# Layer 0's experts in two runs of blocks that take turns, each with a weight buffer loaded where the expert changes

## The chip, the cores and the metric

The kernel runs on one core of a Trainium2 chip. The metric is the device time of one execution in microseconds, the median of a few runs; lower is better. The profile is one execution recorded by the hardware profiler.

## What is computed

The program is a decoder of four layers over 8 x 256 = 2048 tokens of width 256. Each layer has an attention, a cross-attention and a feed-forward part, each with a residual and a LayerNorm behind it. The change touches the feed-forward part of layer 0, a mixture of eight experts where each token goes to one expert:

```python
x_flat = x.reshape(-1, D)                        # 2048 x 256
router_logits = x_flat @ gate_w                  # 2048 x 8
router_probs = softmax(router_logits)
expert_idx = argmax(router_probs)
expert_w = router_probs[expert_idx]
for e in range(8):                               # w1[e]: 256 x 1024, w2[e]: 1024 x 256
    y = gelu(x_flat @ w1[e] + b1[e]) @ w2[e] + b2[e]
    out = out + where(expert_idx == e, expert_w, 0)[:, None] * y
...
x = layernorm(x + out)
```

## The kernel before

The tokens are kept as 16 tiles of 128 (`NT`), in `X` with tokens on the partitions and in `xT` with features there. `l0_ffn` works in three stages.

The router multiplies `xT` by the gate (`plog`), picks the best expert of each token, counts tokens per expert and gives each expert as many blocks of 128 slots as its tokens need. At most `NB` = 16 + 7 = 23 blocks can come up, and the loop always runs over 23. `end` holds the running sum of the blocks, `slot` says at which place each token stands, `take` (from `takers`) says which token stands at each place of each block. `owner` is the expert of each block times 128; blocks behind the last used one belong to expert 7. `wrow` adds the partition's number: it is, for each block, the list of 128 rows of the table `l0f_experts` that hold the weights of the expert. The tokens are also written to DRAM (`xd`).

The second stage is the loop over blocks. For block `n`, GpSimd issues an indirect DMA (`gather_rows`, line 893) that fetches 128 rows of 4360 numbers, the expert's `w1`, `w2`, `b1` and `b2`, into the tile `we`. The pool `f0e` has two buffers, so a load waits until the block before last has done its last read. A second indirect DMA (in `gathered_T`) fetches the 128 tokens of the block into `xe`; TensorE transposes them (`pt`, line 908), ScalarE copies the result to `xeT`. Then TensorE makes eight pieces of the hidden layer (`ph`), ScalarE applies Gelu with the bias `b1` (`hT`, line 999), TensorE multiplies by `w2` (`py`), VectorE adds `b2` (`y`, line 1005, the last read of `we`), and SP writes `y` to `yd` in DRAM. A matrix product in 32-bit floats shows as two matmuls in the trace, so a block has 32 rows of `ph` and 16 of `py`.

The third stage gathers from `yd` the row of each token (`yg`), scales it by the router's weight, adds the residual and normalises (`finish`).

The order of the instructions on each engine is chosen by a scheduler when the program is built; the source gives only the dependences. Each engine's queue runs in its order. On GpSimd's queue the built order is, once the loop has settled, one gather of `xe` and then one of `we`, and in the last seven turns `we` alone. `gather_rows` has an optional bound (`rows`): rows of the index at or above it are dropped and raise no error. Before the change only the lookup of layer 2's table (`rows` from `l2f_table`) passes one.

Of the kernel before, what the change touches and what calls it, by code (L numbers as in the profile page):

```python
# [11 lines left out]
F32 = mybir.dt.float32  # L12
# [4 lines left out]
ALU = mybir.AluOpType  # L17
# [3 lines left out]
P = 128  # L21
B, S, D = 8, 256, 256
# [20 lines left out]
class Net:  # L43
# [874 lines left out]
    def l0_ffn(self, w):  # L918
        nc, tc = self.nc, self.tc
        (gate,) = w  # L920
        E, FC = 8, 8
        NB = NT + E - 1
        with (
            tc.tile_pool(name="f0", bufs=1) as pool,
            tc.tile_pool(name="f0w", bufs=3) as work,
            tc.tile_pool(name="f0e", bufs=2) as ework,
            tc.tile_pool(name="f0d", bufs=1, space=bass.MemoryType.DRAM) as dram,
        ):
            with tc.tile_pool(name="f0r", bufs=1, space=PSUM) as ps:
                plog = ps.tile([P, NT, E], F32, name="plog")  # L930
                for i in range(NT):
                    self.mm(plog[:, i, :], [(self.xT4[:, c, i, :], gate[:, c, :]) for c in range(2)])
                m8, _, oh, pos, cnt = self.route(plog, E, 1, pool, ps)
                pe = pool.tile([P, NT, 8], F32, name="pe")
                nc.vector.tensor_tensor(pe, m8, m8[:, :, 0:1].to_broadcast([P, NT, 8]), ALU.subtract)
                nc.scalar.activation(pe, pe, AF.Exp)
                gw = pool.tile([P, NT], F32, name="gw")
                nc.vector.tensor_reduce(gw, pe, AX.X, ALU.add)
                nc.vector.reciprocal(gw, gw)
                nblk = pool.tile([P, E], I32, name="nblk")  # L940
                nc.vector.tensor_scalar(nblk, cnt, float(P - 1), None, ALU.add)
                nc.vector.tensor_single_scalar(nblk, nblk, 7, ALU.arith_shift_right)
                end = pool.tile([P, E + 1], F32, name="end")
                nc.vector.memset(end[:, 0:1], 0.0)
                for e in range(E):
                    nc.vector.tensor_tensor(end[:, e + 1 : e + 2], end[:, e : e + 1], nblk[:, e : e + 1], ALU.add)
                first = pool.tile([P, E], F32, name="first")
                nc.vector.tensor_scalar(first, end[:, :E], float(P), None, ALU.mult)
                slotf = pool.tile([P, NT, E], F32, name="slotf")
                nc.vector.tensor_tensor(slotf, pos, first.unsqueeze(1).to_broadcast([P, NT, E]), ALU.add)  # L950
            xd = self.in_dram(pool, dram)
            slot1 = self.pick(oh, slotf, 1, E, pool, "slot1")
            slot = pool.tile([P, NT, 1], U32, name="slot")
            nc.vector.tensor_copy(slot, slot1)
            parts = pool.tile([P, 2, NT, 1], I32, name="parts")
            nc.vector.tensor_single_scalar(parts[:, 0], slot.bitcast(I32), 7, ALU.arith_shift_right)
            nc.vector.tensor_single_scalar(parts[:, 1], slot.bitcast(I32), P - 1, ALU.bitwise_and)
            block = pool.tile([P, 2, NT, 1], F32, name="block")
            nc.vector.tensor_copy(block, parts)
            group = pool.tile([P, NT, 1, NB], F32, name="group")  # L960
            nc.vector.tensor_tensor(
                group[:, :, 0, :],
                self.cst("iota")[:, :NB].unsqueeze(1).to_broadcast([P, NT, NB]),
                block[:, 0].to_broadcast([P, NT, NB]),
                ALU.is_equal,
            )
            with tc.tile_pool(name="f0t", bufs=1, space=PSUM) as ps:
                take = self.takers(block[:, 1], group, 1, pool, work, ps, pool)
            past = pool.tile([P, NB, E], F32, name="past")
            nc.vector.tensor_tensor(  # L970
                past,
                self.cst("iota")[:, :NB].unsqueeze(2).to_broadcast([P, NB, E]),
                end[:, 1:].unsqueeze(1).to_broadcast([P, NB, E]),
                ALU.is_ge,
            )
            owner = pool.tile([P, NB], F32, name="owner")
            nc.vector.tensor_reduce(owner, past, AX.X, ALU.add)
            nc.vector.tensor_scalar(owner, owner, float(E - 1), float(P), ALU.min, ALU.mult)
            wrow = pool.tile([P, NB], U32, name="wrow")
            nc.vector.tensor_scalar(wrow, owner, self.cst("part"), None, ALU.add)  # L980
            yd = dram.tile([NB * P, D], F32, name="yd")
            with tc.tile_pool(name="f0p", bufs=2, space=PSUM) as ps:
                for n in range(NB):
                    we = ework.tile([P, 2 * FC * P + FC * D + FC + D], F32, name="we")
                    self.gather_rows(we, self.ins["l0f_experts"], wrow[:, n : n + 1])
                    o = 2 * FC * P
                    w1 = we[:, :o].rearrange("p (c f) -> p c f", c=2)
                    w2 = we[:, o : o + FC * D].rearrange("p (f d) -> p f d", d=D)
                    b1 = we[:, o + FC * D : o + FC * D + FC]
                    b2 = we[:, o + FC * D + FC :]  # L990
                    xeT = self.gathered_T(xd, take[:, n : n + 1], work)
                    hT = work.tile([P, FC, P], F32, name="hT")
                    for g in range(0, FC, 4):
                        ph = ps.tile([P, 4, P], F32, name="ph")
                        for f in range(4):
                            self.mm(
                                ph[:, f, :], [(w1[:, c, (g + f) * P : (g + f + 1) * P], xeT[:, c, :]) for c in range(2)]
                            )
                            nc.scalar.activation(  # L999
                                hT[:, g + f, :], ph[:, f, :], AF.Gelu, bias=b1[:, g + f : g + f + 1]  # L1000
                            )
                    py = ps.tile([P, D], F32, name="py")
                    self.mm(py, [(hT[:, f, :], w2[:, f, :]) for f in range(FC)])
                    y = work.tile([P, D], F32, name="y")
                    nc.vector.tensor_tensor(y, py, b2, ALU.add)  # L1005
                    nc.sync.dma_start(yd[n * P : (n + 1) * P, :], y)
                for i in range(0, NT, 2):
                    z = work.tile([P, 2, D], F32, name="z")
                    for j in range(2):
                        y = work.tile([P, D], F32, name="yg")  # L1010
                        self.gather_rows(y, yd, slot[:, i + j, :])
                        nc.vector.scalar_tensor_tensor(
                            z[:, j], y, gw[:, i + j : i + j + 1], self.X[:, i + j, :], ALU.mult, ALU.add
                        )
                    self.finish(i, 1, z)
# [1023 lines left out]
```

## Time and profile before

| | |
|---|---|
| three timed runs | 2792.59, 2801.1, 2802.07 us; median 2801.1 |
| the profiled execution | 2675.02 us, of which the span of the core is 2673.2 us |
| mean granted TensorE clock in it | 0.883 |
| the loop over blocks in it | first `ph` at 332.4 us, last `y` at 557.2 us |
| loads of `we` in it | 23, each 2.23 MB |
| one gather instruction of `we` on GpSimd | median 942 ns |
| one `y` on VectorE | 424 to 426 ns |

Durations in what follows come from this one execution. A row of the trace gives the start and the length, the engine, the line of the source, the operation and its tiles (output, arrow, inputs), and in brackets how long the engine stood idle before it and what ended that. PE is TensorE, PEld its weight loads, DVE VectorE, ACT ScalarE, POOL GpSimd, SP the engine that issues plain DMAs. A releaser named in brackets is inferred: of several things waited for, it is the one that came last by the profile. The table's lines of code are those of the kernel before.

### The profile page before, as it was taken

The page shows a single profiled execution, that of the slowest core. Times are in us where ns is not written, and L with a number is a line of the kernel's source. Part 1 is how long each engine was busy: PE and PEld are TensorE (multiplying, and loading weights), DVE is VectorE, ACT ScalarE, POOL GpSimd, SP SyncE. Part 2 cuts the span into 40 slices and gives each one's busy share as a digit, 9 for nine tenths or more (in the row PEclk, how much of TensorE's full clock was granted, in tenths as well). Part 3 has the DMA queues.
Part 4 walks back from the last instruction along what each step waited for, and adds up shares of the span by engine and source line. Part 5 has one row for each costly group of instructions (what it writes and reads, how often), then busy time and mean ns, then how long its engine had stood idle before and what let it go on. Part 6 is the DMA issues. An engine that isn't in the chain of part 4 may idle for free.

```text
span 2673.2 us, 40915 instructions
## 1 busy us (share of the span) xinstructions
PE 2156.6 (81%) x14331; PEld 1560.5 (58%) x14331; DVE 1678.8 (63%) x5710; ACT 957.6 (36%) x2197; POOL 890.1 (33%) x949
## 2 busy tenths in 40 slices
PE   8978688869999867854998667888898899878975
PEld 5555477745556546741555425666677677656754
DVE  4754400056666757536676788787797787664876
ACT  2321133323333344211344224345455445433431
POOL 1021121131111112446111003776767766670000
PEclk9998599989998877985999788898999998887987
DMA  2001276720001013743000001212111211220000
GB/s 84 2 1 36 88 255 242 268 76 1 1 1 68 13 43 99 229 147 87 1 1 25 36 0 60 54 52 53 51 48 46 59 46 50 54 75 0 1 20 12
DMA packets 84172, 166.28 MB, mean 62 GB/s; under 512 B 31653, under 2 KB 51253, under 8 KB 80256
## 3 DMA queue, kind: packets, MB, share of 16 engines
q0 software_dynamic: 52288, 110.51, 13.5%
q1 hardware_dynamic: 28924, 49.45, 5.5%
q10 hardware_dynamic: 2756, 3.72, 0.4%
q8 instruction: 114, 1.87, 0.3%
q14 instruction: 90, 0.74, 0.1%
HBM read 242.90 MB, written 17.70 MB: 97 GB/s over the span
## 4 chain that ended last, share of the span: by engine, by line
PE 20%; DVE 17%; DMA 6%; issue 5%; POOL 2%; ACT 2%; POOLq 0%; ACTq 0%; DVEq 0%
DMA rows<-in_l2f_table_dram,index 6%; PE s L132 3%; PE pp L132 3%; PE po L1392 3%; PE po L132 3%; DVE junk L1340 2%; DVE low L478 1%; POOL rows L893 1%; PE ph L132 1%; PE sc L132 1%; PE s L1538 1%; PE sc L445 1%; PE s L1516 1%; DVE X L187 1%; DVE top_i L1216 1%
## 5 line engine op out<-in xcount | busy, mean ns | idle before, releaser
L893 POOL DMA_INDIRECT rows<-in_l2f_table_dram,index x512 | 531.9, 1039 | 227.7 <-issue 68.9
L1340 DVE SCALAR_TENSOR_TENSOR junk<-rows,X 128x256 f32<-128x256 f32 x512 | 215.8, 421 | 145.7 <-DMA rows<-in_l2f_table_dram,index 134.6
L1392 PE MATMUL po<-rows,diag 128*128 128x256 f32 x768 | 218.5, 423 | 43.6 <-ACT diag L1391 41.6
L132 PE MATMUL ph<-xeT,we 128*128 128x128 f32 x1248 | 187.4, 294 | 35.2 <-DMA we<-in_l0f_experts_dram,wrow 31.0
L132 PEld LDWEIGHTS ph<-xeT,we 128*128 128x128 f32 x1248 | 172.8, 204 | 58.5 <-DMA we<-in_l0f_experts_dram,wrow 34.4
L1392 PEld LDWEIGHTS po<-rows,diag 128*128 128x128 f32 x768 | 149.0, 207 | 91.3 <-ACT diag L1391 65.0
L553 POOL TENSOR_TENSOR aT<-sides,inv 128x256 f32<-128x256 f32 x64 | 46.7, 730 | 448.4 <-DVE sides L551 255.8
L132 PE MATMUL pp<-xT,w 128*128 128x256 f32 (+1 forms) x672 | 183.4, 411 | 9.6 <-DVE hT L1028 3.3
L173 PE MATMUL pt<-ident,X 128*128 128x128 f32 x352 | 77.7, 335 | 119.7 <-DVE X L187 105.5
L1391 ACT ACTIVATE diag<-ident,dots 128x128 f32<-128x128 f32 x384 | 133.1, 394 | 103.0 <-DVE dots L1386 62.7
L893 POOL DMA_INDIRECT xe<-xd,take x87 | 85.0, 977 | 221.7 <-DVE y L1005 94.7
L132 PEld LDWEIGHTS pp<-xT,w 128*128 128x128 f32 x672 | 131.9, 203 | 40.2 <-issue 9.4
L174 ACT COPY xT<-pt 128x512 f32<-128x512 f32 x88 | 51.5, 586 | 277.0 <-PE pt L173 276.7
L1005 DVE TENSOR_TENSOR y<-py,we 128x256 f32<-128x256 f32 x23 | 9.8, 425 | 220.3 <-PE py L132 220.3
L141 POOL TENSOR_SCALAR rs_v<-ln_mv 128x2 f32<-128x2 f32 x48 | 12.4, 259 | 389.2 <-DVE ln_mv L164 358.5
L173 PEld LDWEIGHTS pt<-ident,X 128*128 128x128 f32 x352 | 50.2, 165 | 156.7 <-issue 73.3
L132 PE MATMUL py<-we,hT 128*128 128x256 f32 x496 | 132.2, 391 | 0.9 <-DVE hT L1028 0.9
L517 ACT ACTIVATE e<-sc 128x512 f32<-128x512 f32 (+1 forms) x155 | 82.0, 602 | 105.5 <-PE sc L445 92.2
L999 ACT ACTIVATE hT<-ph,we 128x128 f32<-128x128 f32 x184 | 66.0, 367 | 142.8 <-PE ph L132 136.0
L187 DVE TENSOR_SCALAR X<-z,ln_mv,rs_y 128x256 f32<-128x256 f32 x192 | 72.0, 418 | 52.2 <-POOL rs_y L143 52.1
L445 PE MATMUL sc<-kv,qv 32*128 32x128 f32 (+2 forms) x1448 | 101.5, 320 | 2.8 <-DVE sides L551 0.8
L445 PEld LDWEIGHTS sc<-kv,qv 32*128 32x128 f32 x1448 | 78.3, 190 | 37.4 <-issue 30.1
(489 smaller groups left out, 5223.5 us busy)
## 6 DMA issues: line engine op xcount, KB each, us to landing
we<-in_l1f_experts_dram SPq DMA_DIRECT2D x32, 384.0 KB, 4.2
yd<-y SPq DMA_DIRECT2D x32, 256.0 KB, 2.1
rows<-in_l2f_table_dram,index POOLq DMA_INDIRECT x512, 2.8
w<-in_l2x_w_dram SPq DMA_DIRECT2D x1, 4096.0 KB
yd<-y SPq DMA_DIRECT2D x23, 128.0 KB, 1.7
X<-in_x_dram SPq DMA_DIRECT2D x8, 256.0 KB, 7.7
xd<-X ACTq DMA_DIRECT2D x8, 256.0 KB, 2.2
xd<-X SPq DMA_DIRECT2D x8, 256.0 KB, 2.1
```

Of the source, the lines that this page charges most:

```text
L132: self.nc.tensor.matmul(out, lhsT=lhsT, rhs=rhs, start=n == 0, stop=n == last and bias is None)
L173: nc.tensor.transpose(pt[:, c, j, :], self.X[:, i0 + j * step, c * P : (c + 1) * P], self.ident)
L174: nc.scalar.copy(self.xT4[:, :, i0 : i0 + step + 1 : step, :], pt)
L187: nc.vector.tensor_scalar(self.X[:, i, :], z[:, j, :], mv[:, j, 0:1], r[:, j : j + 1], ALU.subtract, ALU.mult)
L445: nc.tensor.matmul(sc[: shape[0], part], lhsT=lhsT, rhs=rhs, start=mask is None, stop=True, skip_group_check=True)
L517: lambda r, sc: nc.scalar.activation(e0[m][:n0, r], sc, AF.Exp),
L553: nc.gpsimd.tensor_tensor(out, split(both), split(inv), ALU.mult)
L893: self.nc.gpsimd.indirect_dma_start(out=out, out_offset=None, in_=table, in_offset=bass.IndirectOffsetOnAxis(ap=index, axis=0), **({} if r ...
L999: nc.scalar.activation(hT[:, g + f, :], ph[:, f, :], AF.Gelu, bias=b1[:, g + f : g + f + 1])
L1340: nc.vector.scalar_tensor_tensor(junk, row, 1.0, self.X[:, i, :], ALU.mult, ALU.mult, accum_out=out)
L1391: nc.scalar.activation(diag, self.ident, AF.Copy, scale=dots[:, k : k + 1])
L1392: nc.tensor.matmul(po, lhsT=diag, rhs=rows[:, k, D:], start=False, stop=g + k == H * K - 2)
```

## The change

The blocks are cut into two runs, 0 to 11 and 12 to 22. The loop takes them in turns: 0, 12, 1, 13 and so on to 22, 11. Each run has a buffer of its own for weights, so the two tiles are allocated once by name instead of by a pool of two. A new vector `same` marks the blocks whose expert is that of the block before them, with the first block of each run unmarked; a million is added to the rows of the marked blocks in `wrow`. The gather is still issued at each turn, now with the bound of 1024 rows (`E * P`), so that the rows of a marked block are dropped and the buffer keeps the weights that it has.

```diff
-            tc.tile_pool(name="f0e", bufs=2) as ework,
...
             nc.vector.tensor_scalar(owner, owner, float(E - 1), float(P), ALU.min, ALU.mult)
+            first = (NB + 1) // 2
+            turns = [n // 2 + n % 2 * first for n in range(NB)]
+            same = pool.tile([P, NB], F32, name="same")
+            nc.vector.tensor_tensor(same[:, 1:], owner[:, 1:], owner[:, : NB - 1], ALU.is_equal)
+            for n in (0, first):
+                nc.vector.memset(same[:, n : n + 1], 0.0)
+            nc.vector.scalar_tensor_tensor(same, same, 1e6, owner, ALU.mult, ALU.add)
             wrow = pool.tile([P, NB], U32, name="wrow")
-            nc.vector.tensor_scalar(wrow, owner, self.cst("part"), None, ALU.add)
+            nc.vector.tensor_scalar(wrow, same, self.cst("part"), None, ALU.add)
+            weights = [pool.tile([P, 2 * FC * P + FC * D + FC + D], F32, name=f"we{n}") for n in range(2)]
...
-                for n in range(NB):
-                    we = ework.tile([P, 2 * FC * P + FC * D + FC + D], F32, name="we")
-                    self.gather_rows(we, self.ins["l0f_experts"], wrow[:, n : n + 1])
+                for turn, n in enumerate(turns):
+                    we = weights[turn % 2]
+                    self.gather_rows(we, self.ins["l0f_experts"], wrow[:, n : n + 1], E * P)
```

## The prediction

> **What bounds the kernel now.** I read the page's rows first, then who waits on the tile of weights, then TensorE and GpSimd in order of time within layer 0's experts, last the clock in short windows.
>
> The whole kernel leans on TensorE (first fence, the page's busy row and its queue row), but this change touches one stage of some 225 us, so the share of the span says nothing of it. The stage is closed off on both sides: the router must be done before the first gather, and the gathers of `yd` wait for every block's result. What is saved inside passes on in full.
>
> ```profile
> PE 2156.6 (81%) x14331; PEld 1560.5 (58%) x14331; DVE 1678.8 (63%) x5710; ACT 957.6 (36%) x2197; POOL 890.1 (33%) x949
> ...
> q0 software_dynamic: 52288, 110.51, 13.5%
> ```
>
> The view of the tile `we` (who waited for it; us, times):
>
> ```profile
>   PE ph L132: 31.0, 12
> ```
>
> In the stage TensorE stands 31.0 us, in 12 waits, for weights to land. In order of time on TensorE (start, length, operation, in brackets the idle time before it):
>
> ```profile
> 382.55 1.83 PE L132 MATMUL ph<-xeT,we 128*128 128x128 f32 x12
> ...
> 390.04 0.38 PE L908 MATMUL pt<-ident,xe 128*128 128x128 f32 x2
> 393.80 2.44 PE L132 MATMUL ph<-xeT,we 128*128 128x128 f32 x12 [3.38 <-DMA we<-in_l0f_experts_dram,wrow]
> ...
> 402.82 0.38 PE L908 MATMUL pt<-ident,xe 128*128 128x128 f32 x2
> 403.04 1.88 PE L132 MATMUL ph<-xeT,we 128*128 128x128 f32 x12
> ...
> 410.58 0.38 PE L908 MATMUL pt<-ident,xe 128*128 128x128 f32 x2
> 413.85 2.33 PE L132 MATMUL ph<-xeT,we 128*128 128x128 f32 x12 [2.89 <-DMA we<-in_l0f_experts_dram,wrow]
> ```
>
> Blocks go in pairs. Where nothing waits, the next block starts 0.22 us after its transposes (402.82 to 403.04), so the block begun at 382.55 costs 7.71 us (390.26). The one begun at 393.80, after a wait, costs 9.24. GpSimd over the same stretch tells why only every second block waits:
>
> ```profile
> 382.99 0.94 POOL L893 DMA_INDIRECT xe<-xd,take  x1 [9.41 <-DVE y L1005]
> 384.23 0.94 POOL L893 DMA_INDIRECT we<-in_l0f_experts_dram,wrow  x1 [0.30 <-ACT hT L999]
> 390.69 0.94 POOL L893 DMA_INDIRECT xe<-xd,take  x1 [5.52 <-DVE y L1005]
> 391.94 0.94 POOL L893 DMA_INDIRECT we<-in_l0f_experts_dram,wrow  x1 [0.31 <-issue]
> ```
>
> A block's last read of its buffer is `y`; then GpSimd issues one `xe` (1.25 us), then the load of the block after next: 1.5 us after TensorE is done (390.42 to 391.94). The load issued at 384.23 lets TensorE go at 393.80, 9.6 us later; over the stage it is 8.5 to 9.7, near the median landing of the view of `wrow`:
>
> ```profile
> DMA to landing us min/median/max: 8.5/9.4/11.0
> ```
>
> So weights are there 1.5 + 9.3 = 10.8 us after a block ends, and the other buffer's block hides 7.7 of it: a wait of about 3. The pair's second load (391.94) has that wait and the slow block above it and is in time.
>
> **The clock: row against rule.** Windows of 10 us (length; busy us and count of PE, PEld, DVE, ACT, POOL; granted clock, DMA share, GB/s):
>
> ```profile
> 380.00:390.00 10.00, 9.94 (x64) 8.90 (x63) 0.42 (x1) 3.73 (x11) 1.88 (x2) 1.00 0.52 172
> 390.00:400.00 10.00, 6.62 (x36) 5.69 (x35) 0.42 (x1) 2.12 (x7) 1.89 (x2) 0.83 0.88 323
> 400.00:410.00 10.00, 9.94 (x64) 8.91 (x63) 0.42 (x1) 4.07 (x12) 1.89 (x2) 1.00 0.49 167
> ```
>
> The clock drops to 0.83 in the window with a wait. The Trainium skill (TensorE: Matmul & The Clock Gate, part 1, the clock gate) says that the array falls to half clock after at least one idle window of about 3.4 us. Nearly all waits here are shorter (1.9 to 3.5 us), so by the rule the clock should hold, and a removed wait would be worth its 2.8 us alone. In the trace 8 of the 11 long waits are followed by a block of 9.1 to 9.3 us in place of 7.6 to 8.0. Some 12 us in all, 1.1 per long wait on average. I take the trace: a wait costs 2.8 + 1.1 = 3.9 us. The rule's figure is used below for the lower end.
>
> **The loop as it is.** From 332.44 (first `ph`) to 557.2 (last `y`) are 224.8 us. 23 blocks at 7.71 are 177.3. The loss of 47.4 is 11 waits at 3.9 (43), one wait of 0.34, and 4 us of cold start and small gaps.
>
> **The change part by part.**
>
> *Which loads go.* The routing that the reference computes from its own inputs sends 254, 328, 280, 369, 208, 236, 135 and 238 tokens to the eight experts: 2, 3, 3, 3, 2, 2, 2, 2 blocks, 19 of 23, and the four spare ones fall to expert 7. Turns alternate between blocks 0 to 11 and 12 to 22, so turns 0, 1, 3, 4, 7, 10, 11, 16 and 22 load and 14 turns do not. A load is 128 x 4360 x 4 B = 2.23 MB: 51.3 MB become 20.1.
>
> *What a gather costs whose rows are all out of range.* Before has no gather of `we` with a bound, but 512 bounded gathers, those of `rows` from `l2f_table`. Filled, they would move 512 x 128 x 2 KB = 134 MB. Queue q0 moved 110.5; less `we` (51.3), 87 `xe` and 80 `yg` of 0.131 MB (21.9), 37.3 are left: 72% of the rows were dropped, and dropped bytes are not moved. A row of these gathers in GpSimd's group, and their landing (the view of `rows`, its first 60 us):
>
> ```profile
> L893 POOL DMA_INDIRECT rows<-in_l2f_table_dram,index x512 | 531.9, 1039 | 227.7 <-issue 68.9
> ...
> DMA to landing us min/median/max: 2.5/2.8/3.3
> ```
>
> A fully skipped gather lies between nothing and a whole load (9.4); I take the near row, 2.8 us to landing and 1.0 us of GpSimd in place of 0.94. It ends 1.5 + 2.8 = 4.3 us after the block and the cover is 7.7, so it costs nothing; it would begin to show from a landing of 6.2 us. The 0.06 us x 23 on GpSimd lies in its idle time (4.2 to 10.6 us before the `xe` of a turn).
>
> *Which waits stay.* A load is still issued only when its own buffer's last block is done, so only one block of the other run covers it: about 3 us of wait, as now. In the built order GpSimd's gathers stand as before, one `xe` ahead of each `we`, none in the last seven. Two loads that follow each other (turns 3 and 4, 10 and 11) behave as today's pair: the second is hidden under the first one's wait and block. Waits stay at turns 3, 7, 10, 16 and 22: five. Laid out at 7.7 us per block they come to 2.9, 3.2, 3.2, 3.2 and 2.5 (the last without `xe` ahead), 15 us, plus 1.1 to 1.5 each for the clock, 6.5: 21.5 us. Six waits and their clock go: 43 - 21.5 = 21.5; with them go the short wait of 0.34 and, six times, the 0.16 by which the next block's start overlaps the end of its transposes (390.26 against 390.42): 22.8.
>
> *What is added.* On VectorE one `tensor_tensor` and one `scalar_tensor_tensor` of 128 x 23 and a `memset` stand in the router's tail (the other `memset` falls where VectorE idles 13 us for `lg`). The near row is `wrow` itself, 0.227 us for one, at 0.12 to 0.2 from start to start: 0.5 us later for `block`, `take` and the first `xe`, which now set the start (TensorE waits there for `xeT`). `wrow` also moves behind four small operations, so the first load is issued about 1.0 us later, at 323.2; it lands near 332.6 and TensorE would start at 332.9 anyway. I put down 0.7 us. The new loads wait on the same things as before: `y`'s read and the earlier load into that buffer.
>
> *Moved elsewhere.* TensorE's, GpSimd's and SP's order is otherwise the same, but for a zero fill after instead of before one LayerNorm step, on ScalarE's queue one DMA after its neighbour, and, early in layer 1's attention, two score matmuls and a copy of `vp` two places later on TensorE and VectorE. I cost these at 0, at most 1 us either way: neighbours of under 1 us swap, and what waits next waits for all of them.
>
> *Sum.* 22.8 - 0.7 = 22 us. Against the profiled execution, 2675.02 us (span 2673.2): 2653. The three timed runs stand at a median of 2801.1, 4.7% above it, and no trace shows where; stretching the saving likewise makes 23. If all of it were a slower TensorE clock (4.7% over its 81% share is 5.8%), a block would be nearer 8.2, each wait 0.5 shorter and the saving about 19. I keep 22: **2779 us**, 0.8% faster.
>
> **The rivals.**
>
> 1. *The waits hardly cost.* By the clock gate's rule, six waits of 2.8 less 0.7 give 16 us, 2785; if in the timed runs blocks of 9 us hide most of each load, 6 x 1.7 - 0.7 gives 9, 2792. For it: the 4.7% not explained. Against it: the 0.83 rows. Chance 0.13.
> 2. *Nothing is skipped*, because the index of a million and more isn't dropped: 23 loads as now, plus 0.7: 2802. Against it: the bytes of q0. 0.04.
> 3. *All waits go*, because a lone load lands earlier than one that crosses others: at most 47 - 4 less 0.7, 42 us, 2759. Against it: the last load of the loop (539.95), alone, still needed 9.5. 0.06.
> 4. *Slower: a skipped gather is dear.* Dropping 128 rows of 17 KB may take as long as moving them. Place: GpSimd's queue and the landing of 14 gathers. It decides from a landing of 6.2 us; at 9.4 the time is that of before; at 12, pairs wait 2.7 us longer, 7 x 2.7 + 0.7 is 20 more: 2821. For it: no fully skipped wide gather is in the trace. Against it: 2.8 us with 72% dropped. Slower by over 0.5%: 0.06, with a bad draw of layer 1's order.
>
> **How the numbers follow.** My sum holds 0.71, with its own range 2771 to 2787 (five to seven waits kept, clock 0 to 1.5). Half a per cent is 14 us (2787), about what a measurement of this kernel can tell from no change. Faster by over that: 0.71 + 0.06 and of rival 1 the 0.01 near 2785: 0.78; within: 0.12 + 0.04 = 0.16; slower 0.06. The range takes in rival 3 and rivals 1 and 2 nearly whole: 2757 to 2799.
>
> **What would show it.** In the profile after: 9 landings of 8.5 to 11 us and 14 near 2.8 for `we`; q0 at about 79 MB; five waits of TensorE for `we`, 14 to 17 us in sum; the loop about 202 us; windows of 1.00 between reloads; GpSimd's bounded gathers at 1.0 us. I am wrong if skipped gathers land after 6 us, if TensorE waits at turns without a load, if more than seven waits stay, or if the loop shrinks and the kernel does not, layer 1 taking it back.

## The result, and the profile after

The changed kernel takes 2773.35 us (2768.91 to 2777.8, 4 runs) against 2801.59 us for the kernel before, timed beside it (2792.59 to 2811.43, 4 runs): a ratio of 0.9904, 95% interval 0.9878 to 0.993. Forecast were 2779 us and 22 us of saving; measured are 28, with an interval of 20 to 34.

One thing must be known to read the numbers. The execution profiled before (2675.02 us) lies far outside the timed runs of the same kernel, the one profiled after (2775.67 us, span 2773.9) lies among its own. The difference of the two spans, 100 us the other way, is not the change: the lookup of layer 2's table, from its first gather to its last, takes 746.7 us in the profile before and 866.8 in the profile after. On the two chips of the experiments below, where the kernel before takes 2678 and 2680 us, the lookup takes 746.2 us with the kernel before and 745.4 with the changed one. So layer 0's stage is compared by its own times, and whole kernels only by runs made side by side.

The page after, busy row, queue row and the group of `ph` (736 of its 1248 matmuls are layer 0's):

```profile
PE 2171.2 (78%) x14331; PEld 1571.3 (57%) x14331; DVE 1681.6 (61%) x5714; ACT 957.4 (35%) x2197; POOL 891.8 (32%) x949
...
q0 software_dynamic: 52288, 79.27, 9.7%
...
L132 PE MATMUL ph<-xeT,we 128*128 128x128 f32 x1248 | 183.7, 291 | 20.9 <-DMA we<-in_l0f_experts_dram,wrow 16.5
```

The busy row has hardly moved; q0 moves 31.2 MB less, which is 14 loads of 2.23 MB. The view of the tile `wrow` (who waited for it; us, times), then rows of TensorE, among them the five that end a wait:

```profile
  PE ph L132: 16.5, 5
```

```profile
355.78 2.08 PE L132 MATMUL ph<-xeT,we 128*128 128x128 f32 x8 [2.43 <-DMA we<-in_l0f_experts_dram,wrow]
...
392.62 2.66 PE L132 MATMUL ph<-xeT,we 128*128 128x128 f32 x12 [4.31 <-DMA we<-in_l0f_experts_dram,wrow]
...
401.69 1.83 PE L132 MATMUL ph<-xeT,we 128*128 128x128 f32 x12
...
420.57 2.95 PE L132 MATMUL ph<-xeT,we 128*128 128x128 f32 x12 [3.31 <-DMA we<-in_l0f_experts_dram,wrow]
...
452.71 1.83 PE L132 MATMUL ph<-xeT,we 128*128 128x128 f32 x12
...
460.42 1.83 PE L132 MATMUL ph<-xeT,we 128*128 128x128 f32 x12
...
471.79 2.95 PE L132 MATMUL ph<-xeT,we 128*128 128x128 f32 x12 [3.50 <-DMA we<-in_l0f_experts_dram,wrow]
...
521.49 2.44 PE L132 MATMUL ph<-xeT,we 128*128 128x128 f32 x12 [2.98 <-DMA we<-in_l0f_experts_dram,wrow]
```

Twelve waits have become five, at turns 3, 7, 10, 16 and 22. Between them a block follows the other in 7.71 us (452.71 to 460.42); after a wait it takes 9.07 (392.62 to 401.69). GpSimd, at a turn that drops its gather and at one that loads:

```profile
446.70 1.01 POOL L893 DMA_INDIRECT we<-in_l0f_experts_dram,wrow  x1 [0.30 <-ACT hT L1008]
...
462.12 1.01 POOL L893 DMA_INDIRECT we<-in_l0f_experts_dram,wrow  x1 [0.30 <-ACT hT L1008]
```

Both hold the queue for 1.01 us. The first is the gather of the block that starts on time at 452.71, the second that of the block whose wait ends at 471.79, 9.7 us after the issue. Windows of 10 us over that wait, in the profile after:

```profile
460.00:470.00 10.00, 8.23 (x54) 7.12 (x52) 0.85 (x2) 3.09 (x9) 2.97 (x3) 1.00 0.69 252
470.00:480.00 10.00, 8.21 (x46) 7.69 (x47) 0.00 (x0) 3.10 (x9) 0.00 (x0) 0.83 0.04 13
480.00:490.00 10.00, 9.88 (x67) 8.76 (x67) 0.85 (x2) 3.83 (x11) 1.92 (x2) 1.00 0.08 25
```

The clock (third number from the right) falls to 0.83 in the window in which the wait ends and is 1.00 in the two beside it. The DMA share falls to 0.04 where nothing is loaded.

### The profile page after: what moved, and what is told of

It reads as the page before. It is cut to its first block, busy times and chain, and to the rows that moved or that the text cites. A ratio compares the mean times of both kernels' runs of the same rounds, so it can differ in the third digit from the quotient of the medians.

```text
span 2773.9 us, 40937 instructions
## 1 busy us (share of the span) xinstructions
PE 2171.2 (78%) x14331; PEld 1571.3 (57%) x14331; DVE 1681.6 (61%) x5714; ACT 957.4 (35%) x2197; POOL 891.8 (32%) x949
## 3 DMA queue, kind: packets, MB, share of 16 engines
q0 software_dynamic: 52288, 79.27, 9.7%
## 4 chain that ended last, share of the span: by engine, by line
PE 25%; DVE 16%; issue 6%; ACT 3%; another core or an unknown queue 2%; POOL 2%; DMA 0%; ACTq 0%; POOLq 0%; DVEq 0%
PE po L1401 5%; PE pp L132 4%; PE s L132 4%; PE po L132 3%; DVE junk L1349 2%; DVE low L478 1%; PE ph L132 1%; PE s L1547 1%; PE sc L132 1%; PE s L1525 1%; POOL rows L893 1%; PE po L1382 1%; PE sc L445 1%; DVE X L187 1%
## 5 line engine op out<-in xcount | busy, mean ns | idle before, releaser
L1401 PE MATMUL po<-rows,diag 128*128 128x256 f32 x768 | 231.2, 437 | 90.7 <-ACT diag L1400 54.4
L132 PE MATMUL pp<-xT,w 128*128 128x256 f32 (+1 forms) x672 | 196.9, 435 | 35.1 <-issue 20.4
L132 PE MATMUL ph<-xeT,we 128*128 128x128 f32 x1248 | 183.7, 291 | 20.9 <-DMA we<-in_l0f_experts_dram,wrow 16.5
L132 PEld LDWEIGHTS pp<-xT,w 128*128 128x128 f32 x672 | 141.6, 218 | 69.2 <-issue 29.7
L445 PE MATMUL sc<-qv,kv 32*128 32x128 f32 (+2 forms) x1396 | 99.1, 347 | 0.0
```

What stands on the lines that cost most here:

```text
L132: self.nc.tensor.matmul(out, lhsT=lhsT, rhs=rhs, start=n == 0, stop=n == last and bias is None)
L445: nc.tensor.matmul(sc[: shape[0], part], lhsT=lhsT, rhs=rhs, start=mask is None, stop=True, skip_group_check=True)
L1401: nc.tensor.matmul(po, lhsT=diag, rhs=rows[:, k, D:], start=False, stop=g + k == H * K - 2)
```

## The experiments

They ran on two chips, four on each, here A and B. The kernel before takes 2677.72 us on A and 2680.0 on B. Each ratio is to runs of the kernel before on the same chip, and the loop is read from the run's own profile, first `ph` to last `y`. The kernel before was profiled again on A alone, the changed one on B alone, so where loops of the two chips are set side by side, some 2 us may be the chip or the execution (two profiles of one kernel differ by 1.9).

| kernel | chip | loads | waits of TensorE for `we`: number, us | loop, us | ratio to before, 95% interval |
|---|---|---|---|---|---|
| before, again | A | 23 | 12, 31.5 | 226.7 | 0.999 (0.9978 to 1.0002) |
| turns, all loads made | A | 23 | 13, 32.1 | 225.9 | 0.9993 (0.9981 to 1.0005) |
| skipping in the old order | B | 16 | 8, 20.4 | 210.1 | 0.9946 (0.9927 to 0.9965) |
| the changed kernel, again | B | 9 | 5, 15.8 | 200.5 | 0.9905 (0.9888 to 0.9923) |
| dropped gathers not issued | A | 9 | 6, 13.1 | 195.9 | 0.9871 (0.9849 to 0.9893) |
| first loads only | A | 2 | 0 | 178.2 | 0.980 (0.978 to 0.982) |
| three runs, three buffers | B | 9 | 0 | 182.0 | 0.9842 (0.9825 to 0.986) |
| before with three buffers | B | 23 | 0 | 182.2 | 0.9823 (0.9805 to 0.9841) |

**The kernel before against itself.**

> The kernel before, unchanged, run as if it were a change: what two equal kernels show against each other, and a second profile of it. Ratio 1.000 within 0.3%. Theory: the loop over layer 0's blocks takes 225 us as in the first profile (12 waits of TensorE for weights, 31 us), and the 120 us by which the profile after is longer than the profile before in layer 2's table stage are no work of the change: this profile shows the stage at about 875 us in place of 755, at an execution near 2800 us. Rival: the change itself slows layer 2's stage (its place in memory, its order); then the stage stays at 755 us here while the timed runs agree with the profile, about 2675 us.

The ratio, 0.999, shows what equal kernels differ by. The expectation of a slow layer 2 failed: here the kernel takes 2674.61 us and the stage 746. The rival, that the change slows layer 2, fell another way: the changed kernel's own profile on chip B has the stage at 745.4 us.

**The turns without the skipping.**

> The changed kernel with the million that marks a block replaced by 0, so that all 23 loads are made; turns, buffers, bound and the added VectorE work are as in the change. Theory (the gain is the waits that skipped loads take with them): 11 or 12 waits of about 3 us come back, loop 225 us, time as before or 1 us more, ratio 1.000 within 0.003. Rival (the order of turns, the fixed buffers or the other built order give the gain): the loop stays near 202 us and the ratio near 0.990.

```diff
-            nc.vector.scalar_tensor_tensor(same, same, 1e6, owner, ALU.mult, ALU.add)
+            nc.vector.scalar_tensor_tensor(same, same, 0.0, owner, ALU.mult, ALU.add)
```

The view of `wrow` in this kernel:

```profile
  PE ph L132: 32.1, 13
...
DMA to landing us min/median/max: 8.5/9.3/10.6
```

The waits are back in full and with them the time. Order, fixed buffers, bound and added VectorE work gain nothing by themselves and cost nothing that can be measured.

**The changed kernel again, on chip B.**

> The changed kernel, unchanged, on the chip of this series, so that it stands beside the experiments and has a second profile. Theory: ratio 0.991, within 0.002; five waits, 16 to 17 us, loop 202 us. If the 28 us of the first comparison (22 were worked out for the loop) came from the loop, the loop here is 5 us shorter or that of before longer; if they came from elsewhere, the ratio here is 0.992.

2652.05 against 2680.0 us. The ratio is that of the first comparison. In the view of `wrow` the landings are there to read:

```profile
  PE ph L132: 15.8, 5
...
DMA to landing us min/median/max: 2.1/2.8/9.2
```

The view counts only gathers whose landing the trace tells, here 15 of 23. Twelve of them are dropped ones, which land in 2.1 to 3.9 us; the longest, 9.2, is a load. The loop here is 26.2 us shorter than that of the kernel before on chip A; in the first pair of profiles it was 22.4 (224.8 to 202.4). So the loop of one and the same kernel differs by about 2 us from one execution to the next, and the few us between 22 forecast and 28 timed lie within what these runs can tell.

**Skipping in the old order.**

> Skipping without the two runs: blocks in the order 0 to 22, alternate buffers, a gather dropped where the block two before has the same expert. 16 loads and 7 dropped gathers in place of 9 and 14. Theory (a wait arises at each load that does not follow directly on a waiting one; the loads' number does not matter by itself): waits at turns 2, 5, 8, 11, 13, 15 and 17, seven of about 3 us plus 1.3 of slow clock, loop about 212 us, ratio 0.9955. Rival (what counts is the bytes or the number of loads): 16 of 23 loads keep their share of the 24 us, saving 7/14 of it, 12 us, loop 213: the two do not part in the time, but in the number and place of the waits, seven at the named turns against eight or more spread as before.

```diff
-            turns = [n // 2 + n % 2 * first for n in range(NB)]
+            turns = range(NB)
...
-            nc.vector.tensor_tensor(same[:, 1:], owner[:, 1:], owner[:, : NB - 1], ALU.is_equal)
+            nc.vector.tensor_tensor(same[:, 2:], owner[:, 2:], owner[:, : NB - 2], ALU.is_equal)
-            for n in (0, first):
+            for n in (0, 1):
```

Seven waits of 2.5 to 3.3 us stand where they were named, at turns 2, 5, 8, 11, 13, 15 and 17. An eighth of 0.23 us is at turn 14, whose load is hidden but for that. The loop came to 210.1 in place of 212. With 16 loads the waits are seven and with 9 they are five, so it is the place of a load that decides: one that directly follows a waiting one is nearly free.

**Dropped gathers not issued.**

> The changed kernel with the gather issued only at the nine turns that load for these inputs (written as a list in the source); the 14 gathers whose rows are all dropped are not issued at all. Theory (a dropped gather costs nothing: 1.0 us of GpSimd in idle time, landing under cover): loop within 2 us of the changed kernel's 202, ratio to before 0.990 within 0.002. Rival (dropped gathers hold GpSimd's queue or TensorE): the loop shrinks by 5 us or more.

```diff
-                    self.gather_rows(we, self.ins["l0f_experts"], wrow[:, n : n + 1], E * P)
+                    if turn in (0, 1, 3, 4, 7, 10, 11, 16, 22):
+                        self.gather_rows(we, self.ins["l0f_experts"], wrow[:, n : n + 1], E * P)
```

The loop is 4.6 to 6.5 us shorter than in the changed kernel's two profiles, about where the rival was to begin, and the ratio of 0.9871 is a little better. But this kernel was built in another order: TensorE's rows show blocks 7.36 us apart (start of one, start of the next):

```profile
449.65 1.05 PE L132 MATMUL ph<-xeT,we 128*128 128x128 f32 x8
450.54 0.27 PE L908 MATMUL pt<-ident,xe 128*128 128x128 f32 x1
...
457.01 1.05 PE L132 MATMUL ph<-xeT,we 128*128 128x128 f32 x8
```

The transposes stand between the matmuls of `ph` here, not in a row ahead of them. Seven such blocks, 0.3 to 0.4 us shorter each, and four at the end, 0.1 shorter each (7.36 in place of 7.49), are 3 us. Its six waits, 13.1 us, are 2.7 less than the changed kernel's five. Blocks of 7.35 us, with the transposes between the `ph`, come up too in the two kernels with three buffers below, where every gather is issued; so they go with the order and not with the missing gathers. That a dropped gather itself has a cost of some tenths of a us is not excluded by this run; that it is dear is, by the landing of 2.1 to 3.9 us.

**First loads only.**

> The changed kernel with every block but the first of each run marked, so that 2 loads are made and 21 gathers are dropped whole. It leaves out the seven reloads: later blocks use the first expert of their run. Theory: the five waits left in the changed kernel (16.5 us) and the slow clock after them (about 6) go too, loop 180 us, 49 us under the kernel before, ratio 0.982. By the clock gate's rule that idle under 3.4 us keeps the clock, only the 16.5 go: loop 186, ratio 0.9845. Rival (a dropped gather is dear): with 21 of them in place of 14 the loop does not shrink below 200.

```diff
-            nc.vector.tensor_tensor(same[:, 1:], owner[:, 1:], owner[:, : NB - 1], ALU.is_equal)
+            nc.vector.tensor_tensor(same[:, 1:], owner[:, 1:], owner[:, : NB - 1], ALU.is_ge)
```

The landings in the view of `wrow` (of dropped gathers alone, for the trace tells neither load's), and then a window of 160 us (columns as above):

```profile
DMA to landing us min/median/max: 2.1/2.3/3.9
```

```profile
340.00:500.00 160.00, 158.63 (x1041) 142.62 (x1040) 8.91 (x21) 64.44 (x187) 37.00 (x38) 1.00 0.12 32
```

No wait is left, the clock is 1.00 for 160 us, and the loop is 178.2. Against the changed kernel's second profile (chip B) that is 22.3 us less, of which the waits were 15.8. The other 6.5 are the slow blocks after them and small gaps. The 186 us that the clock gate's rule gave, the waits gone and no more, are missed by 8.

**Three runs, three buffers.**

> Three runs of blocks (0 to 7, 8 to 15, 16 to 22) and three buffers, each loaded where the expert changes within its run: again 9 loads. Theory (a reload is late because only one block of 7.7 us covers its 10.8): two blocks, 15.4 us, cover it, so the five waits and the slow clock after them go; loop about 180 us, ratio 0.982, as with 2 loads. Rival (the wait comes from the load itself, contention or the queue, whatever the cover): waits at turns 5, 6, 10, 15 and 22 stay near 3 us and the ratio stays near 0.990.

```diff
-            first = (NB + 1) // 2
-            turns = [n // 2 + n % 2 * first for n in range(NB)]
+            first = (0, 8, 16)
+            turns = [first[n % 3] + n // 3 for n in range(NB)]
...
-            for n in (0, first):
+            for n in first:
...
-            weights = [pool.tile([P, 2 * FC * P + FC * D + FC + D], F32, name=f"we{n}") for n in range(2)]
+            weights = [pool.tile([P, 2 * FC * P + FC * D + FC + D], F32, name=f"we{n}") for n in range(3)]
...
-                    we = weights[turn % 2]
+                    we = weights[turn % 3]
```

Nine loads as in the change, and no wait for one: with two blocks of cover none of the reloads is late. The loop is 182.0 us, and 2634.41 us is 18 below the changed kernel.

**The kernel before with three buffers.**

> The kernel before with three buffers in the pool f0e in place of two, all 23 loads kept. Theory (the loop waits for the latency of a load, not for its bytes; windows with two loads under way moved 320 to 350 GB/s, at which 2.23 MB take 6.4 to 7 us, under the 7.7 of a block): nearly all waits go, loop 180 to 186 us, ratio 0.982 to 0.985. Rival (the stage is bound by the 51 MB, at the 235 GB/s of one load at a time): 23 loads of 8.5 to 9.4 us keep it at 200 us or more, ratio 0.990 or above.

```diff
-            tc.tile_pool(name="f0e", bufs=2) as ework,
+            tc.tile_pool(name="f0e", bufs=3) as ework,
```

Who TensorE waited for between 320 and 515 us (us in all, times, longest); then the landings in the view of `wrow`; then a window:

```profile
PE ph L132 <- ACT xeT L910: 4.7, 12, 0.5
PE pt L908 <- DMA xe<-xd,take: 4.2, 1, 4.2
```

```profile
DMA to landing us min/median/max: 8.9/9.4/12.0
```

```profile
340.00:500.00 160.00, 155.99 (x1027) 140.15 (x1026) 8.49 (x20) 66.48 (x186) 36.23 (x39) 1.00 0.84 312
```

All 23 loads are made, they take as long as before (median 9.4 us), and TensorE waits for none. 312 GB/s flow over 160 us, where the kernel before moved 239 in its second profile (320 to 560 us, the loop and its edges). 2629.74 us, ratio 0.9823: one digit gains nearly twice what the change gains. This version and the three runs, whose intervals overlap, both beat the kernel before and the changed one.

## Why the prediction was right

**Which loads go.** Nine loads were worked out from the routing; q0 shows 79.27 MB, as forecast.

**A dropped gather.** Put down at 2.8 us to landing and 1.0 us of GpSimd, from layer 2's gathers with 72% of their rows dropped; measured 2.1 to 3.9 and 1.0, well under the 6.2 us from which it would show. Rivals 2 (nothing is skipped) and 4 (it is dear) are gone.

**Which waits stay.** Five at the turns named, forecast at 15 us in sum, measured 16.5 and 15.8. One term was too small: turn 7, forecast 3.2, took 4.3 in both profiles, its weights being there 10.8 us after the issue. Why that load is late is not shown by any run; a wait as long stands once in each of two kernels that make all loads (4.2 us in the second profile before, 4.5 with the turns), so a load can be that late without any skipping. The loads without an `xe` ahead are those of the last six turns in the trace, not seven; no wait hangs on that. That one block covers a load and a pair shares one wait was the step that carried the sum; the three-buffer kernels and the old order with skipping tested it from both sides.

**The clock.** Forecast 1.1 to 1.5 us per wait, 6.5 in all. The five blocks after waits took 9.01, 9.07, 8.91, 8.89 and 9.23 us (the last to the end of its `py`), 6.6 above five at 7.71. The clock gate's rule in the Trainium skill (TensorE: Matmul & The Clock Gate, part 1), that it takes an idle window of about 3.4 us, is met by two of the five waits before these (4.31 and 3.50); those of 2.43, 3.31 and 2.98 us were followed by slow blocks as well. In the changed kernel's second profile a wait of 2.74 us was not. Its first twelve `ph` took 1.93 us, where the row at 521.49 above has 2.44, and its block 7.75:

```profile
523.27 1.93 PE L132 MATMUL ph<-xeT,we 128*128 128x128 f32 x12 [2.74 <-DMA we<-in_l0f_experts_dram,wrow]
```

Here the measurement decides: waits under 3.4 us mostly, not always, cost the clock. Rival 1 falls with it.

**The front.** Forecast 0.7 us; from the router's logits (`lg`) to the first `ph` it is 22.2 to 22.5 us before and 23.2 to 23.3 after, so 0.9. Its cause was put wrongly. `take` did not come 0.5 us later: 17.2 us after `lg` in both kernels, so the added VectorE operations fell into gaps between dependent ones. What came later is the first load (0.7 us, forecast 1.0), and TensorE then waited longer for the first `xe` (5.2 to 5.3 us in place of 4.2 to 4.4). The load and that gather are under way together; that the later load is what delays it is likely and was not tested.

**The sum.** 22.8 of loop forecast, 22.4 and 26.2 measured in two pairs of profiles. That the first pair comes so near is in part luck. The waits fell by 14.5 us (31.0 to 16.5) where some 16 were forecast, mostly for turn 7's long wait; the rest of the loop fell by 7.9 where some 7 were forecast.

The swaps in layer 1's order, put at 0, show as nothing in the run with all loads (0.9993). But from the last `y` to layer 2's first gather the changed kernel takes 1102.5 and 1103.7 us in its two profiles, the kernel before 1094.7 and 1096.9. So in these executions some 7 us of the loop's gain do not pass on, against what the prediction says of the stage. With the same order the run with all loads takes 1094.5 there and that with first loads only 1095.6, so the order alone does not do it. Why it happens is not shown; the saving of 28 us is that of the timed runs.

Rival 3, all waits gone, was not what the change does, but is what a third buffer does, by more cover and not by an earlier landing: its figure was 42 us less than the kernel before; measured on chip B are 46 and 50.

## What to carry to other kernels

Before removing transfers, work out from release, issue and landing how many blocks must cover one: here 1.5 + 9.3 us against 7.7 means two, and a third buffer was worth nearly twice what dropping 60% of the loads was. Fewer loads helped this loop, which waits for the latency of a load, only by the waits that they happened to take with them, so count the loads that do not follow a waiting one. Where TensorE waits, add the slow block behind each wait; it was 40% on top here.

## What the runs showed that was not expected

The same two kernels were about 121 us longer in the first comparison than on chip B, nearly all of it in layer 2's table lookup (866.8 against 745.4 us with the same changed kernel), and the ratio was the same in both (0.9904 and 0.9905). What makes the lookup longer is not shown. The order in which the matmuls of a block were built goes with 0.35 us of 7.71 (7.36 with the transposes between the `ph`), with no wait in either case.
